# Taking one operation in two halves, one item apart, in an attention kernel on Trainium2

## The chip, the cores and the metric

The kernel runs on one core of one Trainium2 chip. Its engines work in parallel, each through its own queue in order: TensorE (PE in the profile; PEld is its weight load) multiplies matrices into PSUM, ScalarE (ACT) evaluates functions element by element, VectorE (DVE) does element-wise work and reductions, GpSimd (POOL) does more of the same[...], and SyncE (SP) issues transfers. An engine waits for another through semaphores. The metric is the time of one execution on the device, in microseconds (us).

## The reference: what is computed

Two layers over a graph of 3327 nodes with 128 features. The first, cut to its core:

```python
A_norm = A / deg
x = layernorm(x + A_norm @ x @ W_in + AT_norm @ x @ W_out)
```

The second is an attention in which the 128 features are the heads and each head has only eight components:

```python
q = (x @ Wq.T).reshape(d, n, h)      # d = 128 heads, n = 3327, h = 8; k and v likewise
a = einsum('dnh,dmh->dnm', q, k) * scale
a = a + adj + adj
a = softmax(a, axis=2)
out = einsum('dnm,dmh->dnh', a, v).reshape(n, h * d)
x = layernorm(x + out @ Wo.T)
```

So 128 score matrices of 3327 by 3327 are formed, each needs the maximum of every row before its exponentials, and each exponential is used in a product with only nine columns (eight of v and one of ones, for the sum). The adjacency matrix has few entries in a row; their part is added separately.

## The kernel before, in words

The first layer and the projections take about the first 950 us, the last projection and norm the last 330. Between them lies the attention, with which everything here is concerned. It is one long loop whose order of instructions is written out by hand for every engine (`tc.manual_schedule`): each engine takes its instructions in exactly the order in which the Python code issues them.

Two streams are woven into each other.

**The sums.** For each of 32 groups of four heads, each of seven blocks of 512 queries (the last has 255) and each of 26 tiles of 128 keys, the loop forms scores (L748, tile `e_ps`, one PSUM bank each, three buffers), takes the exponential (L758, ScalarE, tile `es`) and, two tiles later, multiplies with v (`products`, L716, into the accumulator `o`, one bank). One pass of the inner loop over `j0` is called a slot here: two heads, so two `e_ps` matmuls e0 and e1, two exponentials exp0 and exp1, and a set of products. A block of 512 queries has 52 slots, the last block 26.

**The maxima.** The row maxima must be known before the exponentials of the same rows, so this stream runs 76 items ahead (`2 * LEAD`; these come first, with no sums between them). An item (`max_item`) is up to two PSUM banks of scores for 128 queries (L550, tile `m`, two banks, two buffers), which VectorE reduces to a column of `mx` (L570). For each 128 queries and four heads there are 13 items, in the order size, sums, four plain, size, sums, four plain, tails (`items_of`). A plain item reduces 1024 columns at once. Two heads of four use a saving: of two keys whose half sum and half difference are stored, the larger score is the half sum plus the size of the half difference. The item "size" has a bank of half differences, whose absolute value ScalarE takes into the SBUF tile `size` (L560), and a plain bank, which VectorE reduces. The item after it, "sums", has a bank of half sums, which VectorE adds to `size` and reduces in one instruction (L564), and another plain bank (L570).

**How they are woven.** Each slot of the sums takes one item of the maxima. `max_item` is a generator; the slot resumes it at four points, so that the order of a slot is:

- TensorE: m bank 0, e0, m bank 1, e1, products
- ScalarE: exp0, (the size, in a size item), exp1
- VectorE: the item's reductions

[...]A matmul that reuses a buffer waits until the buffer's readers are done: e1 of a slot waits for exp0 of the slot before, e0 for exp1 of two slots before, and the first m matmul of an item for the readers of the item two before. Beside all this GpSimd works on the few adjacency entries, one step in every four key tiles.

Of the kernel before, what the change touches and what calls it, by code (L numbers as in the profile page):

```python
# [9 lines left out]
F32 = mybir.dt.float32  # L10
# [3 lines left out]
AF = mybir.ActivationFunctionType  # L14
ALU = mybir.AluOpType
# [5 lines left out]
P = 128  # L21
# [7 lines left out]
NB = 512  # L29
# [14 lines left out]
LOWEST = -3.0e38  # L44
# [22 lines left out]
def gnn_layers(ctx: ExitStack, tc: tile.TileContext, x, adj, adjt, w_in, w_out, wq, wk, wv, wo, out):  # L67


    nc = tc.nc  # L70
# [369 lines left out]
    with c_att as c1:  # L440
        fixed = c1.enter_context(tc.tile_pool(name="fixed", bufs=1))
        q_pool.append(c1.enter_context(tc.tile_pool(name="q_pool", bufs=5)))
        work = c1.enter_context(tc.tile_pool(name="work", bufs=2))
# [95 lines left out]
        sizes = []  # L539

        def max_item(item):

            k, q, i, *banks, kind, dst = item
            m = ps_m.tile([P, MW], F32, name="m")
            tail = N - 3 * MW
            for n, bank in enumerate(banks):
                width = NB if len(bank) == 1 else tail
                for x, (j, c0) in enumerate(bank):
                    at = n * NB + x * NB // 2
                    nc.tensor.matmul(  # L550
                        m[:, at : at + width],
                        q[64 : 64 + KR, j, i * P : (i + 1) * P],
                        k[64 : 64 + KR, j, c0 : c0 + width],
                        start=True,
                        stop=True,
                    )
                yield
            if kind == "size":
                sizes.append(work.tile([P, NB], F32, name="size"))
                taken = nc.scalar.activation(sizes[-1], m[:, :NB], AF.Abs)  # L560
            yield
            if kind == "sums":
                larger = work.tile([P, NB], F32, name="larger")
                nc.vector.tensor_tensor_reduce(  # L564
                    larger, sizes.pop(0), m[:, :NB], scale=1.0, scalar=LOWEST, op0=ALU.add, op1=ALU.max, accum_out=dst[0]
                )
            src = m if kind == "all" else m[:, NB:]
            if kind == "tails":
                src = m.rearrange("p (n c) -> p n c", n=GH)[:, :, :tail]
            reduced = nc.vector.tensor_reduce(dst[-1], src, axis=AX.X, op=ALU.max)  # L570
            if kind == "size":
                tc.declare_no_dep(reduced.ins, taken.ins, reason="they read two banks of one tile")
            yield

        def by_node():
# [117 lines left out]
        with tc.manual_schedule(engines={ENG.PE, ENG.Activation, ENG.DVE, ENG.Pool, ENG.SP}):  # L693

            def next_item():
                item = next(stream, None)
                return max_item(item) if item is not None else iter(())
# [35 lines left out]
            for g in range(NG):  # L733
                for b, (n0, w) in enumerate(BLOCKS):
# [3 lines left out]
                    for t in range(NT):  # L738
                        pt = P if t < NT - 1 else P - (NP - N)
                        e = []  # L740
                        for j0 in range(0, GH, 2 * per):
                            m = next_item()
                            banks = []
# [22 lines left out]
                        size = NB // 2 if 0 < t < NT - 1 else NB  # L766
# [259 lines left out]
```

## Time and profile before

| | us |
|---|---|
| median of three runs | 13530.39 (13528.57 to 13530.69) |
| the profiled execution, its own time | 13540.9 |
| its span, first to last instruction | 13539.2 |
| busy from 1200 to 13200 us (12000): TensorE | 11815.20 |
| ScalarE | 11839.93 |
| VectorE | 11436.32 |
| GpSimd | 5065.88 |

The granted TensorE clock in that stretch is 1.00. In the lists of groups a row gives the line, the engine, the operation, the tile written and those read, the shapes, the count; then the busy time in us and the mean length of one in ns; then the time that the engine sat idle just before such instructions and what ended most of it. In the order of time a row gives start and length in us, then engine, line and operation; where several instructions follow each other in one row, the length spans them all. Lengths of instructions that overlap in an engine's pipeline add up to more than the time they take.

### The profile page before, as it was taken

Reading aid. Unit: us, or ns where it says so; the run is one execution under the profiler, and the core shown is the slowest. Engines: PE = TensorE matmul, PEld = TensorE weight load, DVE = VectorE, ACT = ScalarE, POOL = GpSimd, SP = SyncE. Lnnn points to the kernel's source line nnn. Section 1 sums busy time; section 2 is a strip of 40 time slices with the busy share of each in tenths; the row PEclk is TensorE's granted clock in tenths of the full one; section 3 lists DMA queues with packets and bytes.
Section 4 is the critical chain, followed back from the end, with each engine's and each line's share of the span. In section 5 each row is a group of like instructions: output and inputs, shape, how many; then the busy total and the mean of one; then the engine's idle time right before and its main releaser. Section 6 shows DMA issues by size and latency. Waiting matters only on the chain.

```text
span 13539.2 us, 323799 instructions
## 1 busy us (share of the span) xinstructions
PE 12894.4 (95%) x131844; PEld 3261.1 (24%) x131844; DVE 12646.1 (93%) x16015; ACT 12688.5 (94%) x24120; POOL 5309.1 (39%) x4554
## 2 busy tenths in 40 slices
PE   7669999999999999999999999999999999999996
PEld 3212222222222222222222222222222222222224
DVE  9789999999999999999999999999999999999996
ACT  6449999999999999999999999999999999999994
POOL 0320000004555555555545555555555555554100
PEclk9869999999999999999999999999999999999997
DMA  6653333333334443343333333444433444333203
GB/s 236 182 127 32 30 32 32 30 31 59 63 66 72 72 69 67 67 67 66 62 64 67 67 66 66 72 70 67 66 68 66 68 67 68 64 62 63 36 9 109
DMA packets 2618909, 929.92 MB, mean 69 GB/s; under 512 B 2261889, under 2 KB 2469897, under 8 KB 2610747
## 3 DMA queue, kind: packets, MB, share of 16 engines
q1 hardware_dynamic: 2489338, 410.96, 25.0%
q0 software_dynamic: 124176, 453.33, 12.1%
q10 hardware_dynamic: 3888, 44.82, 0.9%
q8 instruction: 1035, 16.96, 0.6%
q14 instruction: 472, 3.86, 0.1%
HBM read 786.21 MB, written 151.52 MB: 69 GB/s over the span
## 4 chain that ended last, share of the span: by engine, by line
PE 80%; DVE 9%; ACT 5%; DMA 2%; issue 2%; POOL 1%; SPq 1%; DVEq 0%; ACTq 0%; POOLq 0%
PE o L716 38%; PE m L550 35%; PE e_ps L748 5%; DVE mx L570 5%; ACT es L758 4%; DVE larger L564 1%; PE acc L190 1%; DMA q_d<-parts 1%; DVE top_at L200 1%; PE y L800 1%; DVE top_w L199 1%; ACT size L560 0%; SPq L340 0%; DMA kf_d<-flat 0%; POOL prod L636 0%
## 5 line engine op out<-in xcount | busy, mean ns | idle before, releaser
L758 ACT ACTIVATE es<-e_ps 128x512 f32<-128x512 f32 x21632 | 11446.9, 612 | 167.6 <-PE e_ps L748 119.1
L570 DVE TENSOR_REDUCE mx<-m 128x1 f32<-128x1024 f32 (+2 forms) x10816 | 10646.6, 1049 | 79.9 <-PE e_ps L748 44.4
L748 PE MATMUL e_ps<-q_st,k_st 50*128 50x512 bf16 (+1 forms) x23296 | 6815.4, 366 | 109.5 <-ACT es L758 101.5
L550 PE MATMUL m<-k_st,q_st 48*128 48x512 bf16 (+1 forms) x23296 | 6517.5, 367 | 163.7 <-DVE mx L570 84.0
L716 PE MATMUL o<-es,v 128*9 128x256 f32 (+1 forms) x83456 | 6626.0, 389 | 5.2 <-ACT o_sb L725 5.2
L550 PEld LDWEIGHTS <-q_st 48*128 48x128 bf16 x23296 | 1420.0, 94 | 5035.1 <-issue 4898.0
L519 POOL CAST two<-nm 128x16 bf16<-128x16 f32 (+1 forms) x224 | 43.8, 195 | 5742.4 <-DVE nm L513 5742.4
L716 PEld LDWEIGHTS o<-es,v 128*9 128x9 f32 x83456 | 1242.7, 88 | 4351.9 <-issue 4330.4
L564 DVE CUSTOM_DVE_ANT_0 larger<-size,m 128x512 f32<-128x512 f32 x1664 | 1143.9, 687 | 509.7 <-PE e_ps L748 474.5
L748 PEld LDWEIGHTS <-k_st 50*128 50x128 bf16 (+1 forms) x23296 | 1401.7, 95 | 214.7 <-issue 183.0
L560 ACT ACTIVATE size<-m 128x512 f32<-128x512 f32 x1664 | 987.2, 593 | 110.9 <-PE m L550 77.5
L636 POOL TENSOR_TENSOR prod<-qn,near_rows 128x1024 f32<-128x1024 f32 x416 | 986.6, 2372 | 28.4 <-DMA qn<-qf_d 13.0
L682 POOL TENSOR_TENSOR acc<-acc,prod 128x1024 f32<-128x1024 f32 x390 | 885.7, 2271 | 30.6
L681 POOL TENSOR_TENSOR prod<-near_rows,s 128x1024 f32<-128x1024 f32 x390 | 772.0, 1980 | 6.9
L638 POOL TENSOR_TENSOR half<-prod 128x512 f32<-128x512 f32 x416 | 530.1, 1274 | 32.6
L596 POOL DMA_INDIRECT near_rows<-kn_d,near x416 | 417.3, 1003 | 110.6 <-issue 58.9
L596 POOL DMA_INDIRECT near_rows<-vn_d,near x416 | 411.8, 990 | 63.3 <-issue 22.3
L190 PE MATMUL acc<-a_t,x 128*128 128x512 f32 (+1 forms) x728 | 311.5, 585 | 64.4 <-DMA a_t<-in_adj_dram 44.4
L665 POOL TENSOR_TENSOR s<-s,gain 128x2048 f32<-128x2048 f32 x26 | 93.8, 3609 | 693.9 <-ACT s L664 693.9
L640 POOL TENSOR_TENSOR quarter<-half 128x256 f32<-128x256 f32 x416 | 254.5, 612 | 32.6
L188 ACT ACTIVATE unread<-a_t 128x3327 bf16<-128x3327 f32 x52 | 155.0, 2980 | 103.0 <-PE acc L190 38.3
L659 POOL COPY acc<-top 128x128 f32<-128x128 f32 x26 | 10.7, 412 | 466.1 <-DVE top L657 433.8
(151 smaller groups left out, 3467.9 us busy)
## 6 DMA issues: line engine op xcount, KB each, us to landing
q_st<-q_d SPq DMA_DIRECT2D x2304, 32.0 KB
a_t<-in_adj_dram ACTq DMA_DIRECT2D x13, 1663.5 KB
a_t<-in_adj_dram SPq DMA_DIRECT2D x13, 1663.5 KB
a_t<-in_adjt_dram SPq DMA_DIRECT2D x13, 1663.5 KB
a_t<-in_adjt_dram ACTq DMA_DIRECT2D x13, 1663.5 KB
q_d<-parts SPq DMA_DIRECT2D x13, 1536.0 KB
k_d<-parts SPq DMA_DIRECT2D x13, 1536.0 KB
k_st<-k_d SPq DMA_DIRECT2D x32, 623.8 KB
```

The costliest lines, as they stand in the source:

```text
L550: nc.tensor.matmul(m[:, at : at + width], q[64 : 64 + KR, j, i * P : (i + 1) * P], k[64 : 64 + KR, j, c0 : c0 + width], start=True, stop=True,
L560: taken = nc.scalar.activation(sizes[-1], m[:, :NB], AF.Abs)
L564: nc.vector.tensor_tensor_reduce(larger, sizes.pop(0), m[:, :NB], scale=1.0, scalar=LOWEST, op0=ALU.add, op1=ALU.max, accum_out=dst[0])
L570: reduced = nc.vector.tensor_reduce(dst[-1], src, axis=AX.X, op=ALU.max)
L596: nc.gpsimd.indirect_dma_start(rows.rearrange("p d h -> p (d h)"), None, table, bass.IndirectOffsetOnAxis(ap=near[:, t, i : i + 1], axis=0))
L636: nc.gpsimd.tensor_mul(prod, qn, kg)
L638: nc.gpsimd.tensor_add(half, prod[:, :, :4], prod[:, :, 4:])
L681: nc.gpsimd.tensor_mul(prod, vg, share)
L682: nc.gpsimd.tensor_add(acc[:, :, :H], acc[:, :, :H], prod)
L716: nc.tensor.matmul(o[32 * j : 32 * j + VW, c : c + w], v4[:pt, j, t, :], e[j][:pt, c : c + w], start=t == 0, stop=t == NT - 1,)
L748: nc.tensor.matmul(bank[:pt, j, :w], k[: KR + 2, j0 + y * per + j, t * P : t * P + pt], q[: KR + 2, j0 + y * per + j, :w], start=True, sto ...
L758: nc.scalar.activation(es[:pt, :, :w], bank[:pt, :, :w], AF.Exp, scale=2.0)
```

## The change

The size item now takes the absolute value of only the first half of its bank of half differences (256 of 512 columns). The other half is taken in the sums item that follows, at the same place in ScalarE's order (between exp0 and exp1 of that slot). For this, `sizes` now carries the tile `m` of the size item and its reduction along. In the sums item VectorE reduces the plain bank first, and then adds and reduces the half sums, for which both halves of `size` must be there. The second declaration of no dependency says that ScalarE's second half and VectorE's reduction of the size item read different banks of one tile.

```diff
             if kind == "size":
-                sizes.append(work.tile([P, NB], F32, name="size"))
-                taken = nc.scalar.activation(sizes[-1], m[:, :NB], AF.Abs)
+                size = work.tile([P, NB], F32, name="size")
+                taken = nc.scalar.activation(size[:, : NB // 2], m[:, : NB // 2], AF.Abs)
+            if kind == "sums":
+                size, m_size, other = sizes.pop(0)
+                taken = nc.scalar.activation(size[:, NB // 2 :], m_size[:, NB // 2 : NB], AF.Abs)
+                tc.declare_no_dep(taken.ins, other.ins, reason="they read two banks of one tile")
             yield
-            if kind == "sums":
-                larger = work.tile([P, NB], F32, name="larger")
-                nc.vector.tensor_tensor_reduce(
-                    larger, sizes.pop(0), m[:, :NB], scale=1.0, scalar=LOWEST, op0=ALU.add, op1=ALU.max, accum_out=dst[0]
-                )
             src = m if kind == "all" else m[:, NB:]
             if kind == "tails":
                 src = m.rearrange("p (n c) -> p n c", n=GH)[:, :, :tail]
             reduced = nc.vector.tensor_reduce(dst[-1], src, axis=AX.X, op=ALU.max)
             if kind == "size":
                 tc.declare_no_dep(reduced.ins, taken.ins, reason="they read two banks of one tile")
+                sizes.append((size, m, reduced))
+            if kind == "sums":
+                larger = work.tile([P, NB], F32, name="larger")
+                nc.vector.tensor_tensor_reduce(
+                    larger, size, m[:, :NB], scale=1.0, scalar=LOWEST, op0=ALU.add, op1=ALU.max, accum_out=dst[0]
+                )
             yield
```

## The prediction

> **What bounds the kernel now.** I read the page's busy table first, then the costliest groups, then the stretch from 1200 to 13200 us, in which the two attention loops run, and last the order of time in one ordinary cycle. From the page:
>
> ```profile
> PE 12894.4 (95%) x131844; PEld 3261.1 (24%) x131844; DVE 12646.1 (93%) x16015; ACT 12688.5 (94%) x24120; POOL 5309.1 (39%) x4554
> ...
> L758 ACT ACTIVATE es<-e_ps 128x512 f32<-128x512 f32 x21632 | 11446.9, 612 | 167.6 <-PE e_ps L748 119.1
> L570 DVE TENSOR_REDUCE mx<-m 128x1 f32<-128x1024 f32 (+2 forms) x10816 | 10646.6, 1049 | 79.9 <-PE e_ps L748 44.4
> ...
> L564 DVE CUSTOM_DVE_ANT_0 larger<-size,m 128x512 f32<-128x512 f32 x1664 | 1143.9, 687 | 509.7 <-PE e_ps L748 474.5
> ```
>
> Three engines are above 92%, so the shares decide nothing; start times do. One slot is one pass of the inner loop: an item's two m matmul groups, two e_ps matmuls, the products, two exponentials. From one size item (its first matmul at 6042.14) to two items later, TensorE's order of time, without the weight loads, reads (start, length, what):
>
> ```profile
> 6042.14 0.39 PE L550 MATMUL m<-k_st,q_st 48*128 48x512 bf16 x1
> ...
> 6043.23 0.39 PE L550 MATMUL m<-k_st,q_st 48*128 48x512 bf16 x1
> ...
> 6044.31 0.39 PE L550 MATMUL m<-k_st,q_st 48*128 48x512 bf16 x1
> 6044.31 0.39 PE L748 MATMUL e_ps<-q_st,k_st 50*128 50x512 bf16 x1
> 6044.54 0.38 PE L550 MATMUL m<-k_st,q_st 48*128 48x512 bf16 x1
> 6044.71 0.37 PE L748 MATMUL e_ps<-q_st,k_st 50*128 50x512 bf16 x1
> 6045.01 0.62 PE L716 MATMUL o<-es,v 128*9 128x256 f32 x8
> 6045.57 0.39 PE L550 MATMUL m<-k_st,q_st 48*128 48x512 bf16 x1
> ```
>
> TensorE sets the pace: 1.09 us a slot without a gap between its pieces. The third slot takes 1.26: its second e_ps matmul starts 0.17 after its m neighbour instead of together with it. Over the whole trace, start to start by place in the cycle of 13 items, the median slot is 1.088 us and the slot two behind a size item 1.254, both times in the cycle. So ScalarE already takes 0.166 us from TensorE per size item. ScalarE and VectorE, same stretch:
>
> ```profile
> 6043.09 0.59 ACT L560 ACTIVATE size<-m 128x512 f32<-128x512 f32 x1
> 6043.56 0.60 ACT L758 ACTIVATE es<-e_ps 128x512 f32<-128x512 f32 x1
> ...
> 6044.04 1.11 ACT L758 ACTIVATE es<-e_ps 128x512 f32<-128x512 f32 x2
> ...
> 6043.97 0.69 DVE L564 CUSTOM_DVE_ANT_0 larger<-size,m 128x512 f32<-128x512 f32 x1 [0.28 <-PE e_ps L748]
> ```
>
> Call the size item n. ScalarE runs exp0(n) from 6042.60, the size from 6043.09, exp1(n) from 6043.56, exp0(n+1) from 6044.04 to 6044.66. There are three e_ps buffers, so e1(n+2) waits for exp0(n+1): 6044.66 plus 0.05 is the 6044.71 above. Undisturbed, ScalarE needs 0.477 us an exponential, 0.95 a slot, and catches up 0.13 a slot. VectorE needs 1.131 for a plain item (more than a slot), 0.60 for a size item and 0.61 + 0.60 for a sums item; it idles 0.31 us before each L564 and is never far from its limit.
>
> **The Trainium skill.** "Perfetto Trace Analysis", section Optimizing Scalar/DVE Operations: where ScalarE isn't saturated but makes bubbles elsewhere, breaking up its instructions can help; the 0.166 is such a bubble. Its section Optimization Strategy says a bubble that repeats can mean too little PSUM for the next tile; here "PSUM — Partial Sum Buffer", Specifications, gives eight banks of 512 fp32 values, and the pools take all eight (three e_ps, two m of two banks, one o), so m stays double-buffered. "ScalarE: Activation LUTs", section What ACT_TABLE_LOAD costs: 186 ns + 0.833 ns a column, neighbours overlapping by 93: 612 and 399 ns for 512 and 256 columns. The trace has 593 for the size (L560's mean on the page), and for 255 columns the copy of o, right behind an exponential:
>
> ```profile
> 8666.09 0.63 ACT L758 ACTIVATE es<-e_ps 128x512 f32<-128x512 f32 x1
> 8666.56 0.42 ACT L725 COPY o_sb<-o 128x255 f32<-128x255 f32 x1
> 8666.81 1.65 ACT L758 ACTIVATE es<-e_ps 128x512 f32<-128x512 f32 x3
> ```
>
> It ends 0.26 us behind the exponential before it (8666.72 to 8666.98) and holds up the next by 0.25. That is my price of a half; the whole costs 0.49 by the same measure. Splitting therefore adds only some 0.03 to 0.05 us of ScalarE time per size item, about 70 us in all, under cover: ScalarE has 0.13 spare in every other slot.
>
> **The change, part by part.**
>
> 1. *First half in the size slot.* 0.26 to 0.27 instead of 0.49, so exp1(n) and exp0(n+1) end 0.22 earlier: exp0(n+1) at 6044.44. e1(n+2), due at 6044.54, would no longer wait. Gain 0.166 us per size item.
>
> 2. *Second half behind exp0(n+1).* It reads the m tile of item n, waits for nothing, and ends 0.27 after exp0(n+1): 6044.71. This is the costly part. m has two buffers, so item n+2 writes where item n lay, and its first matmul, due at 6044.31, must wait for the last reader. Before, that was the size, over at 6043.68, 0.6 us early; now it is the second half. The order of the built program bears it out: that same matmul waits on ScalarE in both kernels, and in the changed one the two e_ps matmuls behind it lose their ScalarE waits (they keep one on TensorE's own, long-past work), since the first wait now covers exp0(n+1). With 0.05 us from release to start it starts at 6044.76: 0.45 us late. Behind it in TensorE's queue stand all e_ps matmuls and products, so nothing fills the gap. e1(n+2) follows 0.23 later at 6044.99 against 6044.71. Net loss of parts 1 and 2: 0.45 − 0.17 = 0.28 us.
>
> 3. *VectorE's order.* L564 waited for the whole tile (both banks' matmuls) before, so taking the plain bank first delays nothing: the reduction starts about 6043.87 (the two-wait form before cost 0.1). The sum then waits for the half: 6044.76 instead of 6043.97. It ends 6045.45; item n+3, which needs that buffer, is due at 6044.76 + 1.09 = 6045.85. VectorE is free at 6045.37 for item n+2, whose data are there at 6045.40. Cost nothing, covered by the stall of part 2; were that gone, about 0.15 us of VectorE's slack per item. Because TensorE is late, VectorE enters the plain items 0.23 us less behind. That removes small stalls: in the last cycle of each block of queries slots of 1.127 stand where 1.088 would be, four or five times. I take 40 us from the sum for this (0 to 90).
>
> 4. *Extra semaphore instructions.* The two exponentials of slot n+2 get a second wait, on ScalarE's own old work. ScalarE is waiting for TensorE there: nothing, 0.05 us if not covered.
>
> Sum. The loop holds 1652 size items (12 of the 1664 fall in the start-up, where no exponentials stand between the halves). Ordinary ones are 1429. The first cycle of each of the 223 later blocks is different: two slots without products let TensorE run ahead (0.44 us each) and VectorE already holds up item n+3 by ending late (6023.73 in the block near 6020). By the same steps there, the half ends 6023.20, VectorE ends 0.21 later than before, part of it absorbed by the wide products two slots on: 0.13 net, 0.25 in the 32 short blocks. 1429 x 0.28 = 400; 191 x 0.13 + 32 x 0.25 = 33; less 40: +393 us. The profiled execution took 13540.9 us (span 13539.2), 10.5 above the median of the three runs; a difference carries over, so 13530.4 + 393 = 13923, say 13920.
>
> **Rivals.**
> A *(0.70)*: as computed. Own range 13840 to 13995: the half's end is uncertain by 0.05 us (±80).
> B *(0.12)*: the same mechanism, smaller. If the half's latency is the 0.372 that an isolated 256-column copy shows, and VectorE's relief is 90: 1429 x 0.23 + 25 − 90 gives +264, 13795.
> C *(0.11)*: the stall is not paid back: e1(n+2), or VectorE behind the late sum, still loses what it lost before. 1652 x 0.45 = +743 at most, 14270; half paid back, 14080. Against it: exp0(n+1) stands ahead of the half in ScalarE's queue, so it is over when the stall ends, and VectorE has 0.4 us to item n+3.
> D *(0.05)*, the other side: the buffer's release is not the last wait, and only the 0.166 goes. 1429 x −0.166 = −237, 13290. For that the half must be over by 0.05 before 6044.31, that is 0.45 us earlier than I have it; the break-even lies 0.28 earlier. Even with an empty ScalarE queue exp0(n+1) cannot start before its own matmul's data, at about 6043.69 (0.46 behind its slot's start, as in slot n), so it ends at 6044.28 and the half at 6044.55, too late for D.
> No change (0.02) would take gain and stall cancelling.
> That the split isn't carried out is excluded: both halves and the new wait stand in the built order.
>
> **How the numbers follow.** About 0.2% (27 us) is what a measurement of this kernel can tell from none. A, B and the nearer part of C are slower: 0.93. D gives 0.05 faster, 0.02 is left for within. The range takes A whole and most of B, and reaches a little towards C: 13785 to 14010.
>
> **What would show it.** In the profile after: two groups of 1664 on ScalarE with 256 columns, about 380 to 420 ns each; TensorE's idle time before L550's matmuls, released by the size, up from nothing by several hundred us; slots of about 1.53 us one behind each size item, and of 1.09 two behind; TensorE's idle time before e_ps for ScalarE gone. VectorE's idle before the sum moved to a wait for the size. It is wrong if the slot behind a size item stays near 1.1 us (D), or if the next one stays at 1.25 (C).

## The result, and the profile after

The changed kernel takes 14025.7 us (median of four runs, 14018.08 to 14028.98) against 13530.54 beside it: a ratio of 1.036, 95% interval 1.0348 to 1.0372, or 495 us more. The forecast was 13920, with a range up to 14010: the direction and the mechanism were right, the size was too small by a fifth, and the time lies 16 us above the range.

From the page of the kernel after:

```profile
PE 12723.8 (91%) x131844; PEld 3367.2 (24%) x131844; DVE 12857.5 (92%) x16015; ACT 13051.6 (93%) x25784; POOL 5316.0 (38%) x4554
...
DVE 42%; ACT 34%; PE 16%; issue 5%; DMA 2%; SPq 1%; POOL 0%; ACTq 0%; DVEq 0%; POOLq 0%
...
L550 PE MATMUL m<-k_st,q_st 48*128 48x512 bf16 (+1 forms) x23296 | 6538.3, 367 | 926.3 <-ACT size L564 778.9
...
L754 PE MATMUL e_ps<-q_st,k_st 50*128 50x512 bf16 (+1 forms) x23296 | 6597.0, 367 | 3.0 <-ACT es L764 1.6
...
L576 DVE CUSTOM_DVE_ANT_0 larger<-size,m 128x512 f32<-128x512 f32 x1664 | 1143.5, 687 | 355.8 <-ACT size L564 351.4
...
L561 ACT ACTIVATE size<-m 128x256 f32<-128x256 f32 x1664 | 630.3, 379 | 108.1 <-PE m L550 75.5
L564 ACT ACTIVATE size<-m 128x256 f32<-128x256 f32 x1664 | 693.7, 417 | 0.0
```

The corresponding lines of the kernel before:

```profile
PE 80%; DVE 9%; ACT 5%; DMA 2%; issue 2%; POOL 1%; SPq 1%; DVEq 0%; ACTq 0%; POOLq 0%
...
L748 PE MATMUL e_ps<-q_st,k_st 50*128 50x512 bf16 (+1 forms) x23296 | 6815.4, 366 | 109.5 <-ACT es L758 101.5
L550 PE MATMUL m<-k_st,q_st 48*128 48x512 bf16 (+1 forms) x23296 | 6517.5, 367 | 163.7 <-DVE mx L570 84.0
```

TensorE's share of busy time has fallen from 95 to 91%, and before L550's matmuls it now sits idle for 926 us, 779 of them until the second half (L564) is done; it was 164. Before the e_ps matmuls its idle time has gone from 110 us to 3. The sum on VectorE (L576) waits for the second half too. The line of shares is the chain of work that ended last: before, 80% of it was TensorE; now it runs mostly through VectorE and ScalarE, since TensorE's waits lead back to them. TensorE's order of time for an ordinary size item (its first m matmul at 6502.19) and the two items behind it, weight loads left out:

```profile
6502.19 0.39 PE L550 MATMUL m<-k_st,q_st 48*128 48x512 bf16 x1
...
6503.28 0.39 PE L550 MATMUL m<-k_st,q_st 48*128 48x512 bf16 x1
...
6503.82 0.62 PE L722 MATMUL o<-es,v 128*9 128x256 f32 x8
6504.83 0.37 PE L550 MATMUL m<-k_st,q_st 48*128 48x512 bf16 x1 [0.40 <-ACT size L564]
6504.84 0.39 PE L754 MATMUL e_ps<-q_st,k_st 50*128 50x512 bf16 x1
6505.05 0.37 PE L550 MATMUL m<-k_st,q_st 48*128 48x512 bf16 x1
6505.06 0.38 PE L754 MATMUL e_ps<-q_st,k_st 50*128 50x512 bf16 x1
6505.37 0.62 PE L722 MATMUL o<-es,v 128*9 128x256 f32 x8
6505.92 0.39 PE L550 MATMUL m<-k_st,q_st 48*128 48x512 bf16 x1
```

The slot behind the size item takes 1.55 us (6503.28 to 6504.83) instead of 1.09, and in the next one both e_ps matmuls stand beside their m neighbours again: 1.09 instead of 1.25. ScalarE and VectorE in the same stretch:

```profile
6503.15 0.38 ACT L561 ACTIVATE size<-m 128x256 f32<-128x256 f32 x1
6503.41 1.09 ACT L764 ACTIVATE es<-e_ps 128x512 f32<-128x512 f32 x2
6504.36 0.41 ACT L564 ACTIVATE size<-m 128x256 f32<-128x256 f32 x1
6504.63 1.79 ACT L764 ACTIVATE es<-e_ps 128x512 f32<-128x512 f32 x3
...
6503.92 0.69 DVE L570 TENSOR_REDUCE mx<-m 128x1 f32<-128x512 f32 x1 [0.32 <-PE e_ps L754]
6504.81 0.69 DVE L576 CUSTOM_DVE_ANT_0 larger<-size,m 128x512 f32<-128x512 f32 x1 [0.20 <-ACT size L564]
```

The second half runs from 6504.36 to 6504.77; 0.06 later TensorE starts m's next matmul, and 0.04 after the half's end VectorE starts the sum.

### The profile page after: what moved, and what is told of

The parts are those of the page before. It is cut to its first block, busy times and chain, and to the rows that moved or that the text cites. A ratio compares the mean times of both kernels' runs of the same rounds, so it can differ in the third digit from the quotient of the medians.

```text
span 14023.7 us, 328015 instructions
## 1 busy us (share of the span) xinstructions
PE 12723.8 (91%) x131844; PEld 3367.2 (24%) x131844; DVE 12857.5 (92%) x16015; ACT 13051.6 (93%) x25784; POOL 5316.0 (38%) x4554
## 4 chain that ended last, share of the span: by engine, by line
DVE 42%; ACT 34%; PE 16%; issue 5%; DMA 2%; SPq 1%; POOL 0%; ACTq 0%; DVEq 0%; POOLq 0%
DVE mx L570 34%; ACT es L764 25%; PE o L722 6%; PE m L550 6%; DVE larger L576 5%; ACT size L561 4%; ACT size L564 3%; PE e_ps L754 2%; DMA q_d<-parts 1%; PE acc L190 1%; DVE top_at L200 1%; DVE top_w L199 1%; PE y L806 1%; ACT o_sb L731 1%; DVE left L422 0%
## 5 line engine op out<-in xcount | busy, mean ns | idle before, releaser
L764 ACT ACTIVATE es<-e_ps 128x512 f32<-128x512 f32 x21632 | 11953.5, 602 | 292.7 <-PE e_ps L754 151.9
L570 DVE TENSOR_REDUCE mx<-m 128x1 f32<-128x1024 f32 (+2 forms) x10816 | 10808.3, 1052 | 510.7 <-PE e_ps L754 436.6
L550 PE MATMUL m<-k_st,q_st 48*128 48x512 bf16 (+1 forms) x23296 | 6538.3, 367 | 926.3 <-ACT size L564 778.9
L754 PE MATMUL e_ps<-q_st,k_st 50*128 50x512 bf16 (+1 forms) x23296 | 6597.0, 367 | 3.0 <-ACT es L764 1.6
L550 PEld LDWEIGHTS <-q_st 48*128 48x128 bf16 x23296 | 1513.9, 94 | 4860.2 <-issue 4762.5
L576 DVE CUSTOM_DVE_ANT_0 larger<-size,m 128x512 f32<-128x512 f32 x1664 | 1143.5, 687 | 355.8 <-ACT size L564 351.4
L561 ACT ACTIVATE size<-m 128x256 f32<-128x256 f32 x1664 | 630.3, 379 | 108.1 <-PE m L550 75.5
L564 ACT ACTIVATE size<-m 128x256 f32<-128x256 f32 x1664 | 693.7, 417 | 0.0
```

The lines of the kernel that those rows point to most:

```text
L550: nc.tensor.matmul(m[:, at : at + width], q[64 : 64 + KR, j, i * P : (i + 1) * P], k[64 : 64 + KR, j, c0 : c0 + width], start=True, stop=True,
L561: taken = nc.scalar.activation(size[:, : NB // 2], m[:, : NB // 2], AF.Abs)
L564: taken = nc.scalar.activation(size[:, NB // 2 :], m_size[:, NB // 2 : NB], AF.Abs)
L576: nc.vector.tensor_tensor_reduce(larger, size, m[:, :NB], scale=1.0, scalar=LOWEST, op0=ALU.add, op1=ALU.max, accum_out=dst[0])
L754: nc.tensor.matmul(bank[:pt, j, :w], k[: KR + 2, j0 + y * per + j, t * P : t * P + pt], q[: KR + 2, j0 + y * per + j, :w], start=True, sto ...
L764: nc.scalar.activation(es[:pt, :, :w], bank[:pt, :, :w], AF.Exp, scale=2.0)
```

## The experiments

The theory to be tested: the loss is the wait of TensorE for the m buffer, whose last reader now comes one slot later, behind another exponential. Rivals: (A) two smaller ScalarE instructions cost more than one; (B) VectorE's new order costs. The first four ran on one chip, with the kernel before at 13523.29 beside them.

**Both halves in one slot** (A alone).

```diff
-                taken = nc.scalar.activation(sizes[-1], m[:, :NB], AF.Abs)
+                halves = [
+                    nc.scalar.activation(sizes[-1][:, c : c + NB // 2], m[:, c : c + NB // 2], AF.Abs) for c in (0, NB // 2)
+                ]
...
```

> Both halves of the size are taken one behind the other in the size slot, VectorE's order is that of before. My theory (the loss is the wait of TensorE for the m buffer whose last reader now comes one slot later): that wait is not there, ScalarE pays only for one more instruction, two times 0.264 against 0.49 us, so the existing stall two slots behind a size item grows by 0.04 us in some 1430 places: about 57 us more than before, 13560 to 13620, slots of about 1.29 two behind the size and of 1.09 one behind. Rival A (the price of more, smaller ScalarE instructions is the loss): about 14000. Rival B (VectorE's new order is the loss): 13530, unchanged.

Measured: 13618.79, ratio 1.0065 (1.0048 to 1.0082): 96 us. TensorE's order of time here, for the slot two behind a size item:

```profile
6133.61 0.39 PE L550 MATMUL m<-k_st,q_st 48*128 48x512 bf16 x1
6133.61 0.39 PE L751 MATMUL e_ps<-q_st,k_st 50*128 50x512 bf16 x1
6133.84 0.38 PE L550 MATMUL m<-k_st,q_st 48*128 48x512 bf16 x1
6134.07 0.37 PE L751 MATMUL e_ps<-q_st,k_st 50*128 50x512 bf16 x1
...
6134.93 0.39 PE L550 MATMUL m<-k_st,q_st 48*128 48x512 bf16 x1
```

The old stall (TensorE's wait for an exponential in that slot) has grown: the slot's median is 1.316 against 1.254. So each split costs 0.062 us of ScalarE's time, not the 0.04 that I had expected, and over 1430 places that makes 89 us. A is real, but a fifth of the loss, and the changed kernel does not show even that: its slot two behind the size item is at 1.090, since ScalarE catches up while TensorE waits.

**The plain bank first** (B alone): the four lines of the sum are moved behind the reduction, the size stays whole.

> Only VectorE's order in the sums item is changed (plain bank first, then the sum); the size is taken whole in its own slot. My theory: VectorE is not what TensorE waits for in ordinary slots, so 13500 to 13540; slots two behind a size item stay at 1.25. Rival B (the new order is the loss): 13700 to 14000.

Measured: 13509.26, ratio 0.9986 (0.998 to 0.9993). So B is refuted: the new order gains 14 us. VectorE starts the sums item's work 0.64 us into the slot instead of 0.75.

**The wait alone.**

```diff
                 sizes.append(work.tile([P, NB], F32, name="size"))
                 taken = nc.scalar.activation(sizes[-1], m[:, :NB], AF.Abs)
+            if kind == "sums":
+                m_size, other = held.pop(0)
+                touch = work.tile([P, 8], F32, name="touch")
+                taken = nc.scalar.activation(touch, m_size[:, :8], AF.Abs)
+                tc.declare_no_dep(taken.ins, other.ins, reason="they read two banks of one tile")
...
```

> The kernel before, with the size whole in its own slot and VectorE's order unchanged; in the sums slot, where the second half stands in the changed kernel, ScalarE reads eight columns of the size item's m tile into a scratch tile that nobody uses. No work is moved, only the m buffer is held until after the first exponential of the next slot. My theory: that alone costs as much as the change: exp0 of the sums slot ends 1.43 us into it, the touch about 0.1 later, so the slot one behind the size takes about 1.57 and the next 1.09: 13980 to 14080. Rivals A and B: at most the touch's own ScalarE time, 0.07 us in 1650 places, 13530 to 13650.

Measured: 14015.84, ratio 1.0356 (1.0339 to 1.0373), within 0.0004 of the changed kernel's own ratio. From its list of groups:

```profile
L551 PE MATMUL m<-k_st,q_st 48*128 48x512 bf16 (+1 forms) x23296 | 6523.6, 367 | 910.1 <-ACT touch L565 764.8 <-DMA q_st<-q_d 71.0 <-DVE mx L576 57.2
...
L565 ACT ACTIVATE touch<-m 128x8 f32<-128x8 f32 x1664 | 356.2, 214 | 0.0
```

The touch does nothing that anyone uses, yet TensorE waits 765 us for it, and the slot behind the size item takes 1.556 (median). Eight columns read at that place cost as much as the half of 256: it is the time of the read that counts, not the work.

**The buffer wait taken away.** As the changed kernel, but the second half reads a constant SBUF tile; the true second half is left out of the result.

```diff
-                taken = nc.scalar.activation(size[:, NB // 2 :], m_size[:, NB // 2 : NB], AF.Abs)
-                tc.declare_no_dep(taken.ins, other.ins, reason="they read two banks of one tile")
+                nc.scalar.activation(size[:, NB // 2 :], stand_in, AF.Abs)
...
```

> As the changed kernel, but the second half reads a constant SBUF tile instead of m, so that it holds no PSUM buffer; it is still written to the size tile and the sum still waits for it. The second half of the size is thus left out of the result. My theory: TensorE no longer waits for ScalarE before L550, slots one behind the size fall from 1.55 to about 1.09. But the sum on VectorE still starts only about 1.53 us into its slot, without a late TensorE to cover it, so VectorE falls behind by about 0.2 us and m's buffers come free late: 13600 to 13800, all of the rest of the loss in waits of L550's matmuls for VectorE. Rival A (more ScalarE instructions): unchanged at 14020. A simpler reading, in which the buffer wait is everything: 13290.

Measured: 13717.94, ratio 1.0145 (1.012 to 1.017). The slot behind the size item is back at 1.090, and what TensorE mostly waits for before L552's matmuls is now the sum on VectorE (L577), as expected:

```profile
L552 PE MATMUL m<-k_st,q_st 48*128 48x512 bf16 (+1 forms) x23296 | 6427.1, 362 | 302.8 <-DVE mx L577 133.9 <-DMA q_st<-q_d 71.2 <-DVE mx L571 58.8
L577 DVE CUSTOM_DVE_ANT_0 larger<-size,m 128x512 f32<-128x512 f32 x1664 | 1144.7, 688 | 335.2 <-ACT size L566 329.6
```

VectorE's sum starts 1.50 us into its slot, no late TensorE lets VectorE catch up, and most slots now last 1.131, which is VectorE's time for a plain item. So the change makes two waits; in the changed kernel the first hides the second.

The next four ran on another chip, the kernel before at 13560.17.

**Both waits taken away.** In addition, the sum reads a constant tile, so that the size is left out of the result.

```diff
-                    larger, size, m[:, :NB], scale=1.0, scalar=LOWEST, op0=ALU.add, op1=ALU.max, accum_out=dst[0]
+                    larger, stand_in_sum, m[:, :NB], scale=1.0, scalar=LOWEST, op0=ALU.add, op1=ALU.max, accum_out=dst[0]
```

> As the run without the buffer wait, and in addition the sum on VectorE reads a constant tile instead of the size tile, so that nobody waits for the second half: all of ScalarE's work is as in the changed kernel, both waits on its late half are gone. The size is thus left out of the result. My theory: the half moved off ScalarE's busiest place is worth what I had priced (0.166 us in about 1430 places, 237 us, and the 14 of the plain bank first), less the stalls that VectorE, with less time from TensorE to catch up, now adds late in each run of plain items (about 0.085 us per 13 items, 70 us): 13290 to 13400. If the late sum on VectorE is not what is left of the loss in the run without the buffer wait: about 13700 again.

Measured: 13536.32, ratio 0.9988 (0.9975 to 1.0001). This misses the expectation: the loss is gone, but of the gain of 237 us only 24 came, and the interval does not exclude none. TensorE's order of time for the slot two behind a size item, up to the second e_ps matmul of the slot after it (which is at 6100.59):

```profile
6099.12 0.39 PE L554 MATMUL m<-k_st,q_st 48*128 48x512 bf16 x1
6099.12 0.39 PE L757 MATMUL e_ps<-q_st,k_st 50*128 50x512 bf16 x1
6099.35 0.38 PE L554 MATMUL m<-k_st,q_st 48*128 48x512 bf16 x1
6099.35 0.38 PE L757 MATMUL e_ps<-q_st,k_st 50*128 50x512 bf16 x1
...
6100.43 0.38 PE L554 MATMUL m<-k_st,q_st 48*128 48x512 bf16 x1
6100.59 0.37 PE L757 MATMUL e_ps<-q_st,k_st 50*128 50x512 bf16 x1
```

The old stall is gone from the slot two behind the size item (1.087) and stands in the next one: 1.234, a stall of 0.146 instead of 0.166. In its queue ScalarE ends an exponential every 0.49 us, so it gains only 1.09 − 0.98 = 0.11 us on TensorE in a slot. Putting half of the work off by one slot lets it gain 0.11 more, of which the split takes 0.06 back (and 0.02 more in this run, whose half reads SBUF and ends 0.30 behind the instruction before it instead of 0.28). By these figures 0.166 − 0.11 + 0.06 + 0.02 = 0.14 should be left; 0.146 is. ScalarE has to do the work before it has caught up with TensorE, whichever slot the work is in.

**The second half ahead of the exponential.** As the changed kernel, with the activation issued before exp0 of the sums slot.

```diff
+                if kind == "sums" and n:
+                    size, m_size, other = sizes.pop(0)
+                    taken = nc.scalar.activation(size[:, NB // 2 :], m_size[:, NB // 2 : NB], AF.Abs)
+                    tc.declare_no_dep(taken.ins, other.ins, reason="they read two banks of one tile")
                 yield
...
```

> As the changed kernel, but the second half stands in the sums slot ahead of that slot's first exponential instead of behind it. It still reads the m tile one slot later than before. My theory: it ends about 1.0 us into that slot, just before the next slot's m matmuls are due (1.09), so the buffer wait is hidden; exp0 behind it is then as late as with both halves in one slot, so the old stall two slots behind the size stays, at about 0.2: as that run less the 14 of the plain bank first, 13560 to 13640. If reading the m tile one slot later is what costs, wherever the half stands: about 14000.

Measured: 13638.36, ratio 1.0057 (1.004 to 1.0074), 78 us. It still reads the tile of an item that is one slot old, but in ordinary places it ends 1.01 us into its slot, in time for the next one at 1.09, and the slot behind the size item takes 1.088; the slot two behind takes 1.316, as with both halves in one slot. TensorE still waits for the half 203 times, 111 us in all, most of it in the first cycles of the blocks, where a slot without products takes 1.12 instead of 0.44. One place in ScalarE's order is the difference between +78 and +495 us.

**A version that takes work off ScalarE.** VectorE idles 0.31 us on average before the first instruction of a sums item (509.7 us over 1664). It can take a part of the size there, by masking the sign bit behind its reduction in the size slot; the plain bank goes first in the sums item. With half of the columns:

```diff
-                taken = nc.scalar.activation(sizes[-1], m[:, :NB], AF.Abs)
+                taken = nc.scalar.activation(sizes[-1][:, :256], m[:, :256], AF.Abs)
...
+                nc.vector.tensor_scalar(
+                    sizes[-1][:, 256:].bitcast(I32), m[:, 256:NB].bitcast(I32), 0x7FFFFFFF, None, op0=ALU.bitwise_and
+                )
```

> The second half of the size is taken by VectorE (the sign bits masked off) behind its reduction in the size slot, plain bank first in the sums item; ScalarE takes the first half alone. No work is left out. My theory: ScalarE's stall goes (237 us), VectorE's new instruction of 256 columns, about 0.34 us, just fills the idle time before the sums item and makes VectorE the limit: per 13 items 13.6 + 2 x 0.34 = 14.3 us against 14.5 before: 13330 to 13450. Rival: VectorE's idle time there is not really free, 13550 or more.

Measured: 13479.77, ratio 0.9947 (0.993 to 0.9963), 80 us faster, which is less than expected: VectorE is at 97%, and slots of plain items late in a block take 1.13 us, its own time.

With a quarter (384 and 128 columns in place of 256 and 256):

> As the run before this one with a quarter (128 columns) on VectorE and three quarters on ScalarE. No work is left out. My theory: ScalarE's stall falls from 0.166 to about 0.06 us, VectorE's instruction of about 0.2 us fits into its idle time, VectorE stays below the limit: 13300 to 13400. Rival: VectorE's idle time is not really free, 13520 or more.

Measured: 13404.24, ratio 0.9882 (0.9865 to 0.9898), 156 us faster and just above the expected 13400. The size and VectorE's part, in the list of groups with shapes apart:

```profile
L560 ACT ACTIVATE size<-m 128x384 f32<-128x384 f32 x1664 | 807.8, 485 | 110.9 <-PE m L550 46.1 <-DMA q_st<-q_d 33.5 <-DVE mx L565 31.3
...
L568 DVE TENSOR_SCALAR size<-m 128x128 int32<-128x128 int32 x1664 | 465.9, 280 | 32.6 <-ACT size L560 18.5
```

The slot two behind a size item has a median of 1.147, so the stall is 0.06, as priced. The size is shorter by 0.11 us, and nothing has been put off. With VectorE at 96%, a larger part gains less, as the run with half shows.

**The slots of 1.127.** The prediction counted on 40 us from slots of about 1.127 us in the last cycle of each block, taking them for VectorE's. The kernel before has four in a block (medians 1.115, 1.128, 1.126 and 1.127). The first two are gone in the changed kernel (1.09), as with the plain bank first alone: they were VectorE's, for before, the m matmul that ends such a slot starts 0.05 us behind the end of the reduction that frees its buffer. The last two stayed. They belong to the last key tile, which has 127 keys. PEld groups of the kernel before, shapes apart:

```profile
L748 PEld LDWEIGHTS <-k_st 50*128 50x128 bf16 x22400 | 1316.1, 94 | 212.8 <-issue 181.2 <-DMA q_st<-negmax_d 5.6
L748 PEld LDWEIGHTS <-k_st 50*127 50x127 bf16 x896 | 85.7, 132 | 1.9 <-issue 1.7
```

A load of 127 weight columns takes 132 ns, one of 128 takes 94. "TensorE: Matmul & The Clock Gate" of the Trainium skill, section Weight-path perf modes, says that the fast weight load is on when the number of weights is 128 and the type is not fp32; the two rows, in bf16, agree. The experiment loads the padding column too:

```diff
+        for k in k_st:
+            nc.vector.memset(k[: KR + 2, :, N:], 1.0)
...
-                                        bank[:pt, j, :w],
-                                        k[: KR + 2, j0 + y * per + j, t * P : t * P + pt],
+                                        bank[:, j, :w],
+                                        k[: KR + 2, j0 + y * per + j, t * P : (t + 1) * P],
```

> The kernel before, with one change: the score matmuls of the last key tile (127 keys) load 128 columns of k, the last a padding column; the exponentials and products still use 127. It asks whose the slots of 1.127 us at the end of each block are, which the prediction put down to VectorE and which the change left as they were. My theory now: they are TensorE's own, the load of 127 weight columns taking 132 ns where 128 take 94, twice a slot: these slots fall to 1.088, 2 x 0.039 x 192 + 0.039 x 32 = 16 us less, ratio 0.9988. The prediction's reading (VectorE is late there): slots and time unchanged.

Measured, beside 13529.61: 13513.64, ratio 0.9987 (0.998 to 0.9993). In the profile all of these loads are alike, and the last two slots of a block are at 1.088 (the two that were VectorE's stay, at 1.117 and 1.129):

```profile
L750 PEld LDWEIGHTS <-k_st 50*128 50x128 bf16 x23296 | 1368.3, 94 | 216.3 <-issue 189.3
```

Such a slot had been longer by 0.039 us, the difference of one load, though it has two of them.

**Both gains together.**

> The quarter of the size on VectorE with the plain bank first, as in the earlier run, together with the full last tile. No work is left out. My theory: both gains add: 0.988 x 0.9988, ratio 0.987 (0.985 to 0.989). If the slots of 1.127 were VectorE's, no more than 0.988.

Measured: 13355.80, ratio 0.9866 (0.9851 to 0.9881), the fastest version of this study: 174 us under the kernel before.

## Why the prediction was right in kind and short in size

By its own steps, with the loop's time from its first m matmul to its last in both traces (12254.2 and 12742.3 us, 488 more, where the sum gave 393):

- **Part 1, the gain of the first half.** The stall of 0.166 did go in the changed kernel, so the term was right inside the sum. As a reason by itself it was wrong: without the buffer wait that gives ScalarE time, the stall only moves a slot on (a ratio of 0.9988, where rival D's 13290 is 0.982). Following ScalarE's queue one slot further would have shown it. The 0.13 us that ScalarE was said to catch up in a slot had been read from its starts (0.477 apart); its ends are 0.49 apart, which leaves 0.11. And a split costs 0.062 us where the prediction had 0.03 to 0.05, which is not covered either when nothing else makes TensorE wait: with both halves in one slot the kernel lost 96 us.
- **Part 2, the buffer wait.** Confirmed place by place: the slot behind the size item was forecast at about 1.53 and is 1.549, the next at 1.09 and is 1.090. Net 0.297 us in an ordinary place and not 0.28, since the second half ended a little later (a stall of 0.46, not 0.45). 1429 x 0.297 = 424 us where I had 400. The wait alone, with no work moved, makes a loss of the same size (493 us).
- **Part 2, the first cycle of a block.** Mis-sized. I had 0.13 us and expected the rest to be absorbed by the wide products. The medians of six slots from the size item on give 7.500 before and 7.734 after in an ordinary block, 0.235; 0.28 where a new group begins and no longer wait falls among the six (7.33 and 7.61), 0.30 in the short blocks. 160 x 0.235 + 31 x 0.28 + 32 x 0.30 = 56 us where I had 33 (the counts are the prediction's; during the last two blocks no items are left to take, which changes the sum by less than 1 us). In the block that begins at 6470.17 (before: 6020.17, counted from the size item), the second e_ps matmul of the third slot behind the size item starts 4.28 us after that item instead of 4.04: it waits for an exponential whose own matmul now comes behind the buffer wait, so in that block nothing is absorbed.
- **Part 3, VectorE's relief.** This is the step that failed, and the largest single error. VectorE did get the slack (its plain item behind the sums starts 0.63 us into its slot instead of 0.88), but next to no time came of it, where I had taken 40 us off. Of the four slots of about 1.127 late in a block, the slot before its second-last size item and that item's own slot did lose their 0.025 and 0.04. But they had also given ScalarE time: the stall two behind that item had been shorter before (the slot at 1.197 instead of 1.254), and with the plain bank first alone it is back at 1.253. So the four slots from the first of these to the one two behind the item together cost 0.285 us more after the change, on average, where an ordinary place costs 0.297: some 2 us over 191 blocks. The other two long slots were TensorE's own, from the load of 127 columns.
- **Part 3, the rest, and part 4.** The new order costs nothing (it gains 14 us by itself), and the late sum on VectorE is indeed covered by the stall; with the cover gone the kernel is 195 us slower than before, as the run without the buffer wait shows.
- **The rest of the loop.** What is left of the 488 is 8 us. Slots last long now and then, in both kernels and at changing places; in the later trace more of them fall into the first cycles of blocks and fewer elsewhere. What makes them was not looked into.
- **The median.** The profiled execution before was 10 us above the median, the one after was at it (14025.4). I had assumed that the difference carries over, and it did not.

424 + 56 + 8 = 488 of the loop; 10 for the median, less 3 outside the loop, make the 495. Against the forecast of 393 the terms are 24, 23, 40, 8 and 7. The range allowed for the half's end and for more relief, but not for none: the relief was taken near the middle of its bounds instead of at zero.

## What to carry to other kernels

Moving a read of a buffer later moves the buffer's release: before a piece of work is put off, follow who writes that buffer next, and where the reader will stand in its engine's queue then. Putting work off by one slot did not relieve a queue that gains a tenth of a slot per slot (0.11 of 1.09 us); giving part of the work to an engine that idles at that moment did (156 us). And a duration that matches one engine's limit is not yet that engine's: of four slots near VectorE's 1.131 us, two were VectorE's and two were TensorE's. Look for the tile at which it recurs.

## What the runs showed of the hardware that was not expected

- A load of 127 weight columns takes 132 ns against 94 for 128, and a slot with two such loads is 0.039 us longer, which is visible in the total (16 us of 13530).
- Queued ScalarE instructions of 512 columns start every 0.477 us and end every 0.49, so that each is recorded 0.013 longer than the one before it (0.592, 0.605, 0.618 from 6043.09 on in the kernel before). A half of 256 adds 0.276 by its end, so two halves cost 0.06 more than the whole. By the difference of starts (0.264 and 0.477) it seemed 0.05, by the copy of o 0.03; the stall grew by 0.062.
- An activation of eight columns lasts 214 ns but holds ScalarE's queue for only 0.06 to 0.07 us (the next exponential starts 57 ns behind its start, and its own end is 70 ns behind that of the exponential before it).
